# Expert lists in DRAM instead of one-hot products: a Mamba layer and a mixture of experts on one core

## The chip, the core and the metric

The kernel runs on one core of a Trainium2 chip. TensorE (PE; its weight loads are shown as PEld), VectorE (DVE), ScalarE (ACT), GpSimd (POOL) and SyncE (SP) run their own queues of instructions in order and wait for each other through semaphores. The metric is the device time of one execution in microseconds, the median of several runs. The profile comes from one more execution, whose own time is given beside it.

## The reference, cut to what matters

The input is one sequence of 4096 tokens of 256 numbers, all float32. A Mamba-like layer, a residual sum and a layer norm come first; then each token goes to one of 8 experts, chosen by the largest router logit, and a second residual sum and layer norm follow.

```python
xz = x @ W_in                                   # 4096 x 1024: conv_in, gated
conv = silu(conv1d(conv_in, conv_w) + conv_b)   # 4 taps, 512 channels
x_dbl = conv @ W_x                              # delta (1), B (16), C (16)
h = exp(delta * A) * h + delta * B * conv[:16]  # scan over the tokens, 16 states
y = (sum(h * C) + conv * D) * silu(gated)
x1 = layernorm(x + y @ W_out)

expert = argmax(x1 @ Wr.T + br)                 # one of 8 for each token
f = relu(x1 @ W1[expert].T + b1[expert]) @ W2[expert].T + b2[expert]
out = layernorm(x1 + f)
```

The kernel sorts the tokens by expert into blocks of up to 128 (some a little longer), so that each token passes through one expert alone.

## The kernel before, in words

**Rounds.** The tokens are cut into 8 blocks of 512 (`TB`). A block passes through a pipeline of steps, and the string `ROUND` gives the order in which one round emits them; `name.c:k` means step `name`, part `c`, for block `r - k` in round `r`. PE executes exactly in this order (its schedule is manual); the other engines' instructions are ordered by a scheduler by priority, and steps marked `@urgent` come ahead of others there. The steps:

- `project` (L748): product with W_in, 8 chunks of 128 columns, two PE products each (L763). ACT evicts chunks 0 to 3 into `xc` and `acc` (L780, L782), chunks 4 to 7 into `sg` (L778); later it makes `cv` from `acc` (L789).
- `taps` (L731): three DVE operations per chunk for the convolution (L734).
- `gauge` (L798): product with W_x (px, L805) and ACT's copy `pxs`. `gauge_out` (L813): four transposes (pxo, L819), an ACT copy and a chain of small DVE operations that ends in `sr` (L853, L856).
- `scan` (L861): transposes of `sr` (pt, L866), exponential on ACT, the scan on DVE (L870 to L881, ending in `parts_`).
- `gate` (L891): one product (py, L896), then for each of 4 chunks a DVE operation (L898) and a product with `sg` (L902), which is done by DVE for chunks 0, 2, 3 and by POOL for chunk 1 (for the last two blocks DVE does 0 and 3, POOL 1 and 2).
- `look`, `look_out` (L906, L923): the router's product with the rows and its transpose. `look_weights` does the same once with W_out.
- `project_out` (L939): four parts of four products (po, L943), residual sum (L947), squares (L951); after the last part the layer norm (L958 to L964) and the write of the rows to `x1d` in DRAM by SP (L968).
- `choose` (L972): nine small DVE operations that find the expert of each token. `rank` (L998): five small products and small DVE operations give each token a place `at` = expert x 4096 + its rank within the expert. Then one-hots are made: `colh` (L1027, DVE) and four `rowh` (L1032, POOL). `place` (L1038): eight products of 128x128 (pz, L1043) put the token numbers into `lists` in SBUF, which DVE adds up (L1047).
- `blocks_of` (L1052), after blocks 2, 4, 5 and 7, calls `table` (L307): from the counts (pn, L320) it works out on DVE which expert and which row of the lists each of 5, 8, 4 and 22 (with 5 lengthened ones) blocks has: `widx` for the weights (L453), and `pick` (L432), a one-hot of the list's row. `tokens_of` (L1062), one round later, calls `lookup` (L463): two products of `lists` with `pick` (pi, L468), an ACT copy (L473), two DVE operations, and `tidx`, the token numbers of the blocks.

**Expert blocks.** `blocks()` (L691) is a generator of the work of 32 blocks in quarters: `hidden` (ph, L598) twice and `close` (pe, L623) twice, with the transposes of the gathered rows (`turn`, pg, L566), the sum `xs` (L641) and `finish` (r, layer norm, y). From round 7 on the strings `QUARTERS` say how many quarters follow each step of a round; what remains comes after the last round. `prefetch` (L520) issues on POOL the indirect gather of a block's rows (xg, L515) and the indirect load of its expert's weights (we, L533; 128 rows of 4360 float32) into one of 3 buffers, up to two blocks ahead; `scatter` (L659) writes results to the output (L661). `turn(0)` stands in round 6 after `look_out`.

**Queues.** The indirect transfers all go through POOL's DMA queue. The 8 PSUM banks are three for `mm` (project, hidden), three for `o` (gate, project_out, close) and two for `tr` (all the rest).

Of the kernel before, what the change touches and what calls it, by code (L numbers as in the profile page):

```python
# [37 lines left out]
F32 = mybir.dt.float32  # L38
I32 = mybir.dt.int32
BF16 = mybir.dt.bfloat16  # L40
F16 = mybir.dt.float16
AF = mybir.ActivationFunctionType
ALU = mybir.AluOpType
AX = mybir.AxisListType
# [41 lines left out]

NM = NE + 1

O2 = DC * FF
OB = O2 + FC * D  # L90
OC = OB + FC
# [4 lines left out]


ROUND = """
    gauge:1 project.0:0 choose:3 gate:2 project.1:0 taps.0:0 tokens_of:4 look_weights:0
    project.2:0 taps.1:0 project.3:0 gauge_out:1 project_out.0:2 rank:3 taps.2:0  # L100
    project_out.1:2 project_out.2:2 taps.3:0 blocks_of:3 look:0 project.4:0 project.5:0
    look_out:1 project.6:0 scan:1 project_out.3:2 place:3 project.7:0
"""
ROUNDS = 13

QUARTERS = {
    7: "2211020000000200010200001000",
    8: "0001000000101100100000001101",
    9: "1000020000010000100000000110",
    10: "0000001000111000001100003002",  # L110
    11: "0000000000100000000000000000",
    12: "0000000000000000000010000000",
}

LOG_SERIES = (0.33333338, 0.19999444, 0.14308298, 0.1071537, 0.1214478)
# [3 lines left out]
def mamba_moe(  # L119
# [27 lines left out]
    def bank(tag, name, bufs=None):  # L147
        return ps.tile([P, 512], F32, tag=tag, name=name, bufs=bufs)


    x1d = dram.tile([T + 1, D], F32, name="x1d")


    st = {}
# [51 lines left out]
    def load_later():  # L206

        nc.sync.dma_start(wx[:, :, 0:XW], W_x.rearrange("(c p) n -> p c n", p=P))
        nc.sync.dma_start(al, A_log)
        nc.sync.dma_start(dp, D_param)  # L210
        nc.sync.dma_start(woutT, W_outT.rearrange("(c p) n -> p c n", p=P))
        nc.sync.dma_start(wout[:, :, 0:D], W_out.rearrange("(c p) d -> p c d", p=P))
        nc.sync.dma_start(brb, br.to_broadcast([P, NE]))
        nc.sync.dma_start(x1d[T : T + 1, :], lists[0:1, 0:D])

    eps = const.tile([P, 1], F32, name="eps")
    nc.gpsimd.memset(eps, EPS)
# [17 lines left out]
    back = iota([P, NE], [[-1, NE]], NE, 0, "back")  # L235
    part = iota([P, 1], [[0, 1]], 0, 1, "part")

    LH = NE * T // P // P
    lrow = iota([P, LH * P], [[P, LH * P]], 0, 0, "lrow", BF16)
    lcol = iota([P, P], [[1, P]], 0, 0, "lcol", BF16)  # L240
    prow = iota([P, LH], [[P * P, LH]], 0, P, "prow")
# [3 lines left out]
    code = const.tile([P, NT], F32, name="code")  # L245
    for base, at in ((1, 0), (-T // 2, NT // 2)):
        nc.gpsimd.iota(
            code[:, at : at + NT // 2], pattern=[[P, NT // 2]], base=base, channel_multiplier=1,
            allow_small_or_imprecise_dtypes=True,
        )  # L250
    lists = const.tile([P, LH * P], F32, name="lists")
    nc.gpsimd.memset(lists, 0.0)

    oneb = const.tile([P, P], BF16, name="oneb")
    nc.vector.tensor_copy(oneb, ones)
# [3 lines left out]
        channel_multiplier=-1,  # L259
# [47 lines left out]
    def table(b0, nb, columns, rows, early):  # L307


        def small(tag, shape, dtype=F32):  # L310
            return r1.tile([P, *shape], dtype, tag=tag, name=f"{tag}{b0}")
# [115 lines left out]
                row[:, nb:], row_of, float(P), blockoff[:, 0:longer], ALU.add, ALU.add  # L427
            )
        nc.vector.tensor_tensor(row[:, 0:nb], row[:, 0:nb], blockoff[:, 0:nb], ALU.add)
        pick = small("pick", [LH, nb + longer])  # L430
        for h in range(LH):
            nc.vector.tensor_scalar(pick[:, h, :], row, prow[:, h : h + 1], None, ALU.is_equal)  # L432
        eb = small("eb", [nb])
        nc.vector.tensor_reduce(eb, past, AX.X, ALU.add)
        if longer:
# [27 lines left out]
        def lookup():  # L463

            pi = bank("tr", f"pi{b0}", 2)
            n = nb + longer
            for h in range(LH):
                nc.tensor.matmul(  # L468
                    pi[:, 0:n], lhsT=lists[:, h * P : (h + 1) * P], rhs=pick[:, h, :],
                    start=(h == 0), stop=(h == LH - 1),  # L470
                )
            codes = small("codes", [n])
            nc.scalar.copy(codes, pi[:, 0:n])  # L473
            half = small("half", [n])
            nc.vector.tensor_scalar(half, codes, 0.0, -float(T + 1), ALU.is_gt, ALU.mult)
            tidx = const.tile([P, n], I32, name=f"tidx{b0}")
            nc.vector.scalar_tensor_tensor(tidx, codes, float(T), half, ALU.add, ALU.add)
            for b in range(nb):
                index[b0 + b] = rows, tidx[:, order(b0, b)]
            for b, x in LONG.items() if longer else ():  # L480
                further[b] = tidx[:, nb + x : nb + x + 1]
# [408 lines left out]
    @urgent  # L890
    def gate(i):  # L891
        cv, sg = st[i]["cv"], st[i]["sg"]


        py = bank("o", f"py{i}")
        nc.tensor.matmul(py, lhsT=oneb, rhs=upper(slice(0, P)), start=True, stop=True)  # L896
        for c in range(CC):
            nc.vector.scalar_tensor_tensor(  # L898
                cv[:, c, :], cv[:, c, :], dp[:, c : c + 1], py, ALU.mult, ALU.add
            )  # L900
            eng = nc.vector if c in ((0, 3) if i >= NB - 2 else (0, 2, 3)) else nc.gpsimd
            eng.tensor_tensor(sg[:, c, :], cv[:, c, :], sg[:, c, :], ALU.mult)  # L902

    rxs = {}
# [67 lines left out]
    def choose(i):  # L972
# [22 lines left out]
        nc.vector.tensor_tensor(earlier[:, i + 1, :], earlier[:, i, :], here, ALU.add)  # L995
        st[i]["oh"], st[i]["best"] = oh, best

    def rank(i):  # L998
        oh, best = st[i]["oh"], st[i]["best"]


        pr = bank("tr", f"pr{i}", 2)
        prv = pr[:, 0 : JT * NE]
        nc.tensor.matmul(
            prv, lhsT=trib, rhs=oh.rearrange("p j e -> p (j e)"), start=True, stop=False
        )
# [12 lines left out]
        at = a2.tile([P, JT], I32, tag="at", name=f"at{i}")  # L1019
        nc.vector.tensor_copy(at, best)  # L1020
        col = a2.tile([P, JT], I32, tag="col", name=f"col{i}")
        nc.vector.tensor_scalar(col, at, P - 1, None, ALU.bitwise_and)
        row = a2.tile([P, JT], F32, tag="row", name=f"row{i}")
        nc.vector.tensor_tensor(row, best, col, ALU.subtract)  # L1024
        rowh = a2.tile([P, JT, LH * P], F16, tag="rowh", name=f"rowh{i}", bufs=1)
        colh = a2.tile([P, JT, P], F16, tag="colh", name=f"colh{i}", bufs=1)
        nc.vector.tensor_tensor(  # L1027
            colh, lcol.unsqueeze(1).to_broadcast([P, JT, P]),
            col.unsqueeze(2).to_broadcast([P, JT, P]), ALU.is_equal,
        )  # L1030
        for j in range(JT):
            (nc.vector if i >= NB - 0 else nc.gpsimd).tensor_scalar(  # L1032
                rowh[:, j, :], lrow, row[:, j : j + 1],
                code[:, i * JT + j : i * JT + j + 1], ALU.is_equal, ALU.mult,
            )
        st[i]["rowh"], st[i]["colh"] = rowh, colh

    def place(i):  # L1038
        rowh, colh = st[i]["rowh"], st[i]["colh"]
        pz = bank("tr", f"pz{i}", 2)  # L1040
        for h in range(LH):
            for j in range(JT):
                nc.tensor.matmul(  # L1043
                    pz[:, h * P : (h + 1) * P], lhsT=rowh[:, j, h * P : (h + 1) * P],
                    rhs=colh[:, j, :], start=(j == 0), stop=(j == JT - 1),
                )
        nc.vector.tensor_tensor(lists, lists, pz[:, 0 : LH * P], ALU.add)  # L1047

    lookups = {}

# [16 lines left out]
    def have(i):  # L1067
# [5 lines left out]
    steps = dict(  # L1073
        project=project, taps=taps, gauge=gauge, gauge_out=gauge_out, scan=scan, gate=gate,
        look=look, look_out=look_out, project_out=project_out, choose=choose, rank=rank,
        place=place, blocks_of=blocks_of, tokens_of=tokens_of,
    )
    for r in range(ROUNDS):
        if have(r + 1):
# [75 lines left out]
```

## Time and profile before

| | |
|---|---|
| median of 3 runs | 474.22 us (473.63 to 474.29) |
| the profiled execution | 473.77 us, span 472.1 us |
| PE clock granted | 0.998 |
| busy share of the span | PE 97%, PEld 73%, DVE 69%, ACT 50%, POOL 40% |
| round from 99.8 to 126.2 us | PE 25.97 of 26.40 us, DVE 23.25, ACT 22.49, POOL 7.64 |
| expert blocks, 280 to 330 us | PE 49.63 of 50.00 us, DVE 30.94, POOL 25.56, DMA share 0.92, 342 GB/s |

A line of PE's waits has the waiting instruction, what ended the wait, then us in total, times, longest. A line of the timeline has start and length in us, engine, line, operation, tiles (out<-in), shape and count; PE's operations overlap, so what one costs is read from start to start. A line of the groups has count, busy us, mean ns of one, idle time before it and what ended that.

### The profile page before, as it was taken

How to read it: one execution, taken by the hardware profiler on the slowest of the kernel's cores; microseconds unless marked ns; L12 is line 12 of the kernel's file. 1: busy time of each engine (PE TensorE's matmuls, PEld its weight loads, DVE VectorE, ACT ScalarE, POOL GpSimd, SP SyncE). 2: the span in 40 equal slices, each digit the busy share in tenths (PEclk: the TensorE clock that was granted, in tenths of full speed). 3: DMA queues.
4: the chain of work that ended last, by engine and by line, in shares of the span. 5: the costliest groups of instructions: out<-in, count | busy, mean ns of one | idle time of the engine just before them, and what ended most of it. 6: DMA issues, size and time to landing. Idle time of an engine off the chain costs nothing.

```text
span 472.1 us, 7486 instructions
## 1 busy us (share of the span) xinstructions
PE 458.8 (97%) x2575; PEld 344.9 (73%) x2576; DVE 326.0 (69%) x1034; ACT 234.2 (50%) x513; POOL 190.1 (40%) x195
## 2 busy tenths in 40 slices
PE   8998999999999899999999999999999999999994
PEld 6343646464564567786888898999989898989884
DVE  2586969797999967984989679544556565645453
ACT  4687898879789784665754331221212121212111
POOL 3000101414154723450575655435436366645541
PEclk9999999999999999999999999999999999999999
DMA  8401012120408906714288499899996189967910
GB/s 247 162 0 46 0 46 89 43 92 1 135 1 345 376 25 206 282 34 184 47 288 279 191 309 356 303 354 345 339 361 248 47 281 357 293 246 248 361 37 22
DMA packets 23401, 89.98 MB, mean 191 GB/s; under 512 B 4914, under 2 KB 14909, under 8 KB 19650
## 3 DMA queue, kind: packets, MB, share of 16 engines
q0 software_dynamic: 8752, 74.71, 43.5%
q1 hardware_dynamic: 13650, 14.50, 9.3%
q8 instruction: 21, 0.34, 0.3%
q10 hardware_dynamic: 960, 0.27, 0.3%
q14 instruction: 18, 0.15, 0.1%
HBM read 87.78 MB, written 9.43 MB: 206 GB/s over the span
## 4 chain that ended last, share of the span: by engine, by line
PE 70%; DVE 17%; ACT 5%; issue 3%; DMA 3%; POOL 1%; POOLq 0%; ACTq 0%; DVEq 0%
PE ph L598 23%; PE pe L623 21%; PE pm L763 12%; PE po L943 7%; DVE acc L734 6%; DMA xg<-x1d,tidx 3%; PE px L805 2%; PE pf L634 1%; PE pg L566 1%; ACT acc L782 1%; DVE xb L947 1%; DVE hT L609 1%; DVE sg L902 1%; ACT xc L780 1%; PE pt L866 1%
## 5 line engine op out<-in xcount | busy, mean ns | idle before, releaser
L763 PE MATMUL pm<-xTb,win 128*128 128x512 f32 (+1 forms) x264 | 119.0, 589 | 0.0
L598 PEld LDWEIGHTS ph<-xgT,we 128*128 128x128 f32 x864 | 100.5, 192 | 3.9 <-DVE r L648 1.3
L598 PE MATMUL ph<-xgT,we 128*128 128x128 f32 x864 | 102.9, 276 | 0.1
L623 PE MATMUL pe<-we,hT 128*128 128x256 f32 x432 | 99.3, 380 | 0.7 <-DVE hT L609 0.7
L623 PEld LDWEIGHTS pe<-we,hT 128*128 128x128 f32 x432 | 79.3, 190 | 11.9 <-DVE hT L609 2.0
L763 PEld LDWEIGHTS pm<-xTb,win 128*128 128x128 f32 x264 | 48.0, 192 | 50.8 <-issue 48.0
L734 DVE SCALAR_TENSOR_TENSOR acc<-xc,cw,acc 128x512 f32<-128x512 f32 x96 | 70.1, 747 | 16.6 <-ACT acc L782 16.2
L285 ACT ACTIVATE sdm<-mvm,eps 128x1 f32<-128x1 f32 x32 | 9.4, 293 | 123.2 <-DVE mvm L283 123.2
L943 PE MATMUL po<-wout,sg 128*128 128x265 f32 x256 | 61.8, 389 | 0.3 <-POOL sg L902 0.3
L533 POOL DMA_INDIRECT we<-in_experts,widx x32 | 34.3, 1072 | 64.9 <-DVE r L648 37.5
L1032 POOL TENSOR_SCALAR rowh<-lrow,row,code 128x256 f16<-128x256 bf16 x32 | 43.9, 1378 | 25.0 <-DVE row L1024 17.9
L943 PEld LDWEIGHTS po<-wout,sg 128*128 128x128 f32 x256 | 46.8, 190 | 8.2 <-POOL sg L902 0.7
L661 POOL DMA_INDIRECT out<-y,tidx x32 | 33.4, 1043 | 44.5 <-DVE y L287 24.9
L609 DVE TENSOR_SCALAR hT<-ph,we 128x128 f32<-128x128 f32 x108 | 31.6, 342 | 25.3 <-PE ph L598 25.1
L902 POOL TENSOR_TENSOR sg<-cv,sg 128x512 f32<-128x512 f32 x10 | 15.7, 1573 | 76.9 <-DVE cv L898 76.8
L648 DVE TENSOR_TENSOR r<-pe,xs 128x256 f32<-128x256 f32 x32 | 13.5, 422 | 44.0 <-PE pe L623 44.0
L515 POOL DMA_INDIRECT xg<-x1d,tidx x32 | 33.2, 1038 | 24.3 <-PE pg L566 12.1
L607 ACT ACTIVATE hT<-ph,we 128x128 f32<-128x128 f32 x108 | 31.0, 366 | 19.6 <-PE ph L598 12.8
L780 ACT COPY xc<-pm 128x512 f32<-128x512 f32 x32 | 18.7, 583 | 21.3 <-PE pm L763 21.3
L782 ACT ACTIVATE acc<-pm,cb,cw 128x512 f32<-128x512 f32 x32 | 25.0, 781 | 0.0
L951 ACT ACTIVATE sta<-xb 128x256 f32<-128x256 f32 x32 | 16.1, 502 | 17.1 <-DVE xb L947 16.9
L947 DVE TENSOR_TENSOR xb<-po,xb 128x265 f32<-128x265 f32 x32 | 13.5, 425 | 15.3 <-PE po L943 15.2
(225 smaller groups left out, 616.0 us busy)
## 6 DMA issues: line engine op xcount, KB each, us to landing
xb<-in_x SPq DMA_DIRECT2D x8, 512.0 KB, 4.9
x1d<-x SPq DMA_DIRECT2D x8, 512.0 KB, 4.8
xTb<-in_xT SPq DMA_DIRECT2D x7, 512.0 KB, 3.7
win<-in_W_in SPq DMA_DIRECT2D x1, 512.0 KB, 5.1
we<-in_W_outT SPq DMA_DIRECT2D x1, 512.0 KB, 5.8
wout<-in_W_out SPq DMA_DIRECT2D x1, 512.0 KB, 6.8
we<-in_experts,widx POOLq DMA_INDIRECT x32
xg<-x1d,tidx POOLq DMA_INDIRECT x32
```

Of the source, the lines that this page charges most:

```text
L515: nc.gpsimd.indirect_dma_start(out=to, out_offset=None, in_=x1d[0:rows, :], in_offset=bass.IndirectOffsetOnAxis(ap=at, axis=0),)
L533: nc.gpsimd.indirect_dma_start(out=wes[n][:, :], out_offset=None, in_=experts, in_offset=bass.IndirectOffsetOnAxis(ap=weights[n], axis=0), ...
L598: nc.tensor.matmul(ph[:, n * w : (n + 1) * w], lhsT=we[:, at : at + P], rhs=xgT[:, dc * w : (dc + 1) * w], start=(dc == 0), stop=(dc == DC ...
L607: nc.scalar.activation(hT[:, fc, :], ph[:, n * w : (n + 1) * w], AF.Relu, bias=bias)
L609: last[b] = nc.vector.tensor_scalar(hT[:, fc, :], ph[:, n * w : (n + 1) * w], bias, 0.0, ALU.add, ALU.max)
L623: nc.tensor.matmul(py[:, 0:D], lhsT=hT[:, fc, 0:P], rhs=out_weights(fc), start=(fc == 0), stop=(fc == FC - 1),)
L661: moved = nc.gpsimd.indirect_dma_start(out=out, out_offset=bass.IndirectOffsetOnAxis(ap=at, axis=0), in_=rows, in_offset=None, bounds_chec ...
L734: nc.vector.scalar_tensor_tensor(acc, xc[:, c, k : k + TB], cw[:, c, k : k + 1], acc, ALU.mult, ALU.add)
L763: nc.tensor.matmul(banks[c][:, at], lhsT=win[:, dc, c * P : (c + 1) * P], rhs=xTb[:, dc, at], start=(dc == 0), stop=(dc == DC - 1),)
L782: evicted = nc.scalar.activation(acc, pm, AF.Identity, scale=cw[:, c, KC - 1 : KC], bias=cb[:, c : c + 1])
L943: nc.tensor.matmul(po[:, 0 : D + NM], lhsT=sg[:, c, j * P : (j + 1) * P], rhs=wout[:, c, :], start=(c == 0), stop=(c == CC - 1),)
L1032: (nc.vector if i >= NB - 0 else nc.gpsimd).tensor_scalar(rowh[:, j, :], lrow, row[:, j : j + 1], code[:, i * JT + j : i * JT + j + 1], AL ...
```

## The change

The lists move to DRAM. `lists` is a DRAM tensor of 257 rows of 128 words, filled once with the number 4096 (a row of zeros in `x1d`) by an SP transfer in `load_later`. `rank` ends with four indirect transfers from POOL, each of which writes 128 token numbers to the places `at`; they are declared free of order among themselves. The one-hots, `place` and its products are gone. `table` makes the number of the list's row on the partition of its block (three DVE operations) and issues on POOL an indirect gather of the rows, `entries`, one partition for each block. `lookup` turns them into float (`numbers`, DVE), transposes them on PE (pi) and copies them to `tidx` (DVE).

The steps of a round stand in a new order, `choose` belongs to the end of the round before, `rank` is urgent, `QUARTERS` is new, and there is one round less. The gate's product on POOL is chunk 0 instead of chunk 1, and for the last two blocks DVE does all four.

```diff
+    lists = dram.tile([LROWS * P, 1], I32, name="lists")
...
 ROUND = """
-    gauge:1 project.0:0 choose:3 gate:2 project.1:0 taps.0:0 tokens_of:4 look_weights:0
-    project.2:0 taps.1:0 project.3:0 gauge_out:1 project_out.0:2 rank:3 taps.2:0
-    project_out.1:2 project_out.2:2 taps.3:0 blocks_of:3 look:0 project.4:0 project.5:0
-    look_out:1 project.6:0 scan:1 project_out.3:2 place:3 project.7:0
+    project.0:0 gauge:1 gate:2 project.1:0 tokens_of:4 taps.0:0 gauge_out:1 taps.1:0
+    project.2:0 project.3:0 taps.2:0 project_out.0:2 taps.3:0 rank:3 project_out.1:2
+    project_out.2:2 blocks_of:3 look_weights:0 project.4:0 project.5:0 look_out:1
+    project.6:0 scan:1 project_out.3:2 choose:2 look:0 project.7:0
 """
-ROUNDS = 13
+ROUNDS = 12
...
-    7: "2211020000000200010200001000",
-    8: "0001000000101100100000001101",
-    9: "1000020000010000100000000110",
-    10: "0000001000111000001100003002",
-    11: "0000000000100000000000000000",
-    12: "0000000000000000000010000000",
+    7: "030001202020010100010001000",
+    8: "001000000010110110000000021",
+    9: "100001011000101000000001001",
+    10: "000000000000110000110000222",
+    11: "000100000000000000000000000",
...
+        nc.sync.dma_start(lists.rearrange("(p n) one -> p (n one)", p=P), noone)
...
-        pick = small("pick", [LH, nb + longer])
-        for h in range(LH):
-            nc.vector.tensor_scalar(pick[:, h, :], row, prow[:, h : h + 1], None, ALU.is_equal)
+        n = nb + longer
+        own = small("own", [n])[0:n, :]
+        nc.vector.tensor_tensor(own, row[0:n, :], ident[0:n, 0:n], ALU.mult)
+        line = small("line", [1])[0:n, :]
+        nc.vector.tensor_reduce(line, own, AX.X, ALU.add)
+        lineno = small("lineno", [1], I32)[0:n, :]
+        nc.vector.tensor_scalar(lineno, line, 1.0 / P, float(LROWS - 1), ALU.mult, ALU.min)
+        entries = small("entries", [P], I32)[0:n, :]
+        nc.gpsimd.indirect_dma_start(
+            out=entries, out_offset=None,
+            in_=lists.rearrange("(r c) one -> r (c one)", c=P),
+            in_offset=bass.IndirectOffsetOnAxis(ap=lineno, axis=0),
+        )
...
-            n = nb + longer
-            for h in range(LH):
-                nc.tensor.matmul(
-                    pi[:, 0:n], lhsT=lists[:, h * P : (h + 1) * P], rhs=pick[:, h, :],
-                    start=(h == 0), stop=(h == LH - 1),
-                )
-            codes = small("codes", [n])
-            nc.scalar.copy(codes, pi[:, 0:n])
-            half = small("half", [n])
-            nc.vector.tensor_scalar(half, codes, 0.0, -float(T + 1), ALU.is_gt, ALU.mult)
+            numbers = small("numbers", [P])[0:n, :]
+            nc.vector.tensor_copy(numbers, entries)
+            nc.tensor.transpose(pi[:, 0:n], numbers, ident[0:n, 0:n])
             tidx = const.tile([P, n], I32, name=f"tidx{b0}")
-            nc.vector.scalar_tensor_tensor(tidx, codes, float(T), half, ALU.add, ALU.add)
+            nc.vector.tensor_copy(tidx, pi[:, 0:n])
...
-            eng = nc.vector if c in ((0, 3) if i >= NB - 2 else (0, 2, 3)) else nc.gpsimd
+            eng = nc.vector if c in ((0, 1, 2, 3) if i >= NB - 2 else (1, 2, 3)) else nc.gpsimd
...
+    @urgent
     def rank(i):
...
-        nc.vector.tensor_tensor(
-            colh, lcol.unsqueeze(1).to_broadcast([P, JT, P]),
-            col.unsqueeze(2).to_broadcast([P, JT, P]), ALU.is_equal,
-        )
         for j in range(JT):
-            (nc.vector if i >= NB - 0 else nc.gpsimd).tensor_scalar(
-                rowh[:, j, :], lrow, row[:, j : j + 1],
-                code[:, i * JT + j : i * JT + j + 1], ALU.is_equal, ALU.mult,
-            )
-        st[i]["rowh"], st[i]["colh"] = rowh, colh
-
-    def place(i):
...
-                nc.tensor.matmul(
-                    pz[:, h * P : (h + 1) * P], lhsT=rowh[:, j, h * P : (h + 1) * P],
-                    rhs=colh[:, j, :], start=(j == 0), stop=(j == JT - 1),
-                )
-        nc.vector.tensor_tensor(lists, lists, pz[:, 0 : LH * P], ALU.add)
+            moved = nc.gpsimd.indirect_dma_start(
+                out=lists, out_offset=bass.IndirectOffsetOnAxis(ap=at[:, j : j + 1], axis=0),
+                in_=tokenno[:, i * JT + j : i * JT + j + 1], in_offset=None,
+            )
+
+            tc.declare_no_dep(moved.ins, group="lists", reason="tokens have no place in common")
+            tc.add_to_no_dep_group("lists", moved.ins)
```

More of the change, by code (lines that the diff above doesn't have):

```diff
@@ L40 @@
 BF16 = mybir.dt.bfloat16
-F16 = mybir.dt.float16
 AF = mybir.ActivationFunctionType
@@ L87 @@
 NM = NE + 1
+LROWS = NE * T // P + 1
 O2 = DC * FF
@@ L213, in load_later @@
         nc.sync.dma_start(brb, br.to_broadcast([P, NE]))
-        nc.sync.dma_start(x1d[T : T + 1, :], lists[0:1, 0:D])
+        nc.sync.dma_start(x1d[T : T + 1, :], parts_[P - 1 : P, 0:D])
+        nc.sync.dma_start(lists.rearrange("(p n) one -> p (n one)", p=P), noone)
     eps = const.tile([P, 1], F32, name="eps")
@@ L236, in mamba_moe @@
     part = iota([P, 1], [[0, 1]], 0, 1, "part")
[L238 to L241, printed above, removed]
     blockno = iota([P, NSB], [[P, NSB]], 0, 0, "blockno")
     blockoff = iota([P, NSB], [[P, NSB]], OFF, 0, "blockoff")
[L245 to L249, printed above, removed]
-        )
-    lists = const.tile([P, LH * P], F32, name="lists")
-    nc.gpsimd.memset(lists, 0.0)
+    tokenno = iota([P, NT], [[P, NT]], 0, 1, "tokenno", I32)
+    noone = iota([P, LROWS], [[0, LROWS]], T, 0, "noone", I32)
     oneb = const.tile([P, P], BF16, name="oneb")
@@ L1020, in rank @@
         nc.vector.tensor_copy(at, best)
[L1021 to L1026, printed above, removed]
-        nc.vector.tensor_tensor(
-            colh, lcol.unsqueeze(1).to_broadcast([P, JT, P]),
-            col.unsqueeze(2).to_broadcast([P, JT, P]), ALU.is_equal,
-        )
         for j in range(JT):
-            (nc.vector if i >= NB - 0 else nc.gpsimd).tensor_scalar(
-                rowh[:, j, :], lrow, row[:, j : j + 1],
-                code[:, i * JT + j : i * JT + j + 1], ALU.is_equal, ALU.mult,
-            )
-        st[i]["rowh"], st[i]["colh"] = rowh, colh
-    def place(i):
[L1039 to L1043, printed above, removed]
-                    pz[:, h * P : (h + 1) * P], lhsT=rowh[:, j, h * P : (h + 1) * P],
-                    rhs=colh[:, j, :], start=(j == 0), stop=(j == JT - 1),
-                )
-        nc.vector.tensor_tensor(lists, lists, pz[:, 0 : LH * P], ALU.add)
+            moved = nc.gpsimd.indirect_dma_start(
+                out=lists, out_offset=bass.IndirectOffsetOnAxis(ap=at[:, j : j + 1], axis=0),
+                in_=tokenno[:, i * JT + j : i * JT + j + 1], in_offset=None,
+            )
+            tc.declare_no_dep(moved.ins, group="lists", reason="tokens have no place in common")
+            tc.add_to_no_dep_group("lists", moved.ins)
     lookups = {}
@@ L1075, in mamba_moe @@
         look=look, look_out=look_out, project_out=project_out, choose=choose, rank=rank,
-        place=place, blocks_of=blocks_of, tokens_of=tokens_of,
+        blocks_of=blocks_of, tokens_of=tokens_of,
     )
```

## The prediction

> **What bounds the kernel now.** I read the page's busy shares first, then the waits of PE, then PE's timeline round by round.
>
> ```profile
> PE 458.8 (97%) x2575; PEld 344.9 (73%) x2576; DVE 326.0 (69%) x1034; ACT 234.2 (50%) x513; POOL 190.1 (40%) x195
> PE   8998999999999899999999999999999999999994
> ```
>
> PE is busy in every slice. Busy is not peak, so I looked for standing time in PE's waits:
>
> ```profile
> PE idle L225 <- POOL ident masks.py:199: 1.6, 1, 1.6
> PE pg L566 <- DMA xg<-x1d,tidx: 1.4, 1, 1.4
> PE py L896 <- DVE parts__145 L881: 1.2, 2, 0.9
> PE pt L866 <- DVE sr L856: 1.2, 3, 0.5
> PE pe L623 <- DVE hT L609: 0.7, 2, 0.4
> PE ph L598 <- DVE r L648: 0.6, 1, 0.6
> PE po L943 <- POOL sg L902: 0.3, 1, 0.3
> ```
>
> After its start PE stands 5.4 us in all; the last 6 us or so are the tail (last layer norm and scatter), which the change leaves alone. So the time is PE's sum of work: a product that leaves PE is a gain, and a new wait in front of a PE instruction is a loss.
>
> The stretch 99.8 to 126.2 is one round: PE 25.97 of 26.40 us, DVE 23.25, ACT 22.49. PE sets it; DVE and ACT have 3 to 4 us spare.
>
> **Removed from PE.** What a step costs is the distance from its first start to the next step's:
>
> ```profile
> 115.75 0.61 PE L1043 MATMUL pz<-colh,rowh 128*128 128x128 f16 x8
> 116.19 1.94 PE L763 MATMUL pm<-xTb,win 128*128 128x512 f32 x4
> ...
> 149.47 0.51 PE L468 MATMUL pi<-pick,lists 128*128 128x5 f32 x4
> 149.83 3.68 PE L763 MATMUL pm<-xTb,win 128*128 128x512 f32 x8
> ```
>
> `place`: 0.44 us, eight times: 3.5 us. Lookup products: 0.36 us, four times; in their place one transpose each, at most 0.11 (the two of pg take 0.38 in all and 0.21 to 0.22 start to start). Gain 4 x 0.25 = 1.0. Together 4.5 us that nothing hides.
>
> **Off DVE, ACT, POOL.** `rank` and `place` lose per round colh 0.68, lists 0.42, col and row 0.16 each on DVE: 1.4 us. Nothing on PE gets shorter by it, but it pays for what follows. POOL trades four rowh for four scatters a round:
>
> ```profile
> L661 POOL DMA_INDIRECT out<-y,tidx x32 | 33.4, 1043 | 44.5 <-DVE y L287 24.9 <-DVE hT L609 4.6 <-DVE spare L441 3.4
> L1032 POOL TENSOR_SCALAR rowh<-lrow,row,code 128x256 f16<-128x256 bf16 x32 | 43.9, 1378 | 25.0 <-DVE row L1024 17.9 <-DVE q L847 7.0
> ```
>
> No scatter of single words is in the trace; the nearest row is this scatter of 128 rows, 1.04 us plus the 0.3 us that POOL shows between two issues: 4 x 1.34 = 5.4 against 4 x 1.38 = 5.5. Bounds: 0.90 (the shortest scatter) to 1.82 us (the longest indirect issue, we), so -0.5 to +3 us of POOL per round. In rounds 3 to 5 nobody waits for it: POOL is busy 7.64 of 26.40 us there.
>
> The Trainium skill speaks against this ("SBUF — State Buffer", Who interferes with whom, and A bandwidth-pool intuition that's wrong): DVE and GpSimd share a port pair, and GpSimd writes no DMA descriptors while DVE holds it; it tells of a 620 ns DMA that took 3100 ns. By that figure four scatters would take about 12 us, the lookups would come some 7 us late each, and the kernel would be slower. The rows show a mild form: xg issues took 1.22 to 1.44 us beside a full DVE (153 to 159 us) against 0.97 at the median. I keep the rows.
>
> **New order of the steps.** `gauge_out` moves forward past project.2 and project.3 (3.4 us), with its ACT copies, its exp table load and 18 small DVE operations; `scan` stays after project.6. So pt, which waits for sr at the end of that chain, gets 3.4 us where it was at most 0.5 late: its 1.2 us go. Late next is py, which waits for DVE's scan chain; between pt and py now stands `look` too (0.57 us), so about half of its 1.2 us go: 0.6. `gauge` has project.0 ahead of it, whose evictions keep ACT busy before pxs; PE reaches the transposes of pxs 1.97 us (py and project.1) after px, the copy takes 0.58: hidden, and 0.6 us a round if ACT is two evictions behind. `choose` goes to the end of the round before, the same place on DVE (nine operations of 0.19 us, right behind the scan chain); `rank` turns urgent; `look` goes behind project_out. The gate's POOL product is chunk 0 instead of 1, and none for the last two blocks: two more DVE products of 0.77 us in each of rounds 8 and 9. The fill of the lists is one more transfer (132 KB) on SP ahead of load_rows; rows are wanted some 40 us later. Fewer rounds: the same quarters of expert work, in other places. All these: nothing on PE unless named.
>
> **The new wait.** Each lookup now goes scatters, gather of `entries`, copy `numbers` on DVE, transpose on PE, tidx, gather of xg. On POOL a weight load stands right before `entries`, and transfers of that queue land in order, as the trace shows for xg behind three weight loads. First stretches of time (their length, POOL busy, clock, DMA share, GB/s), then a line of the chain of waits:
>
> ```profile
> 142.00:143.00 1.00, 0.69 (x2) 1.00 0.00 0
> 143.00:146.00 3.00, 0.91 (x1) 1.00 0.91 291
> 146.00:149.00 3.00, 0.00 (x0) 1.00 1.03 439
> ...
> 153.01 12.19 DMA xg<-x1d,tidx
> ```
>
> A load (128x4360 f32, 2.23 MB) issued at 141.0 moves data from 143 to about 149: 8 us. So `entries` lands some 8.5 us after the load before it is issued, if the queue is empty then; 12.2 us is the other end. `numbers` stands in DVE's queue: while it waits, everything behind it (relus, gate) waits, and PE behind those. The four places, from pn on PE (start of the table), by the order in which the built program issues on each engine, with the durations above and 1.78 per half `hidden`, 1.73 per half `close`:
> - First (round 5 to 6): PE has 15.4 us between pn and the transpose. Scatters and load are issued by about 5.5, landing 14. Late 0 to 0.5; I take 0.3. In return xg0 is no longer behind three loads: turn(0) comes 13 us after the lookup, only one load is ahead of the gather; the 1.4 us go.
> - Second (7 to 8): PE 17.6 us, the load goes out when widx is ready, 3.3; landing 12, DVE is there at 11: 0.3.
> - Third (8 to 9): PE only 11.7 us. POOL has scatters, y3 and xg8 first, load at 3.5, landing 12: late 0.5. Then the gate of block 7, all on DVE: 4 x 0.74 + 4 x 0.77 = 6 us, PE has 5.4 us of other work: 0.9 with what DVE does before it.
> - Fourth (10 to 11): PE 16.2 us. Table on DVE 10 to 11 us (12.8 in the trace less colh and later relus), load at 6.7, landing 15.2: 0.2.
>
> Sum of new waits 2.2 us; bounds 0 and, at 12.2 us from issue to landing against some 6 us of cover each, 24.
>
> **The sum.** The profiled execution took 473.77 us (span 472.1 and 1.7 around it); the median of the three runs is 474.22, 0.45 above. Off: 4.5 products, 1.4 pg, 1.2 pt, 0.6 py = 7.7. On: 2.2, and 0.3 for evictions on ACT. 473.77 - 7.7 + 2.5 = 468.6; against the median 469.0. I forecast 468.6.
>
> **Rivals.**
> 1. Slower: `entries` comes late in all four places. Its place is numbers on DVE; it decides from 7.7/4 = 1.9 us beyond the cover, a landing 8 us after its own issue. For it: 12.19 us in the trace. Against: that one had two full loads and a part of a third ahead, these one. At 9.2 us, 3 late each: 473.8 - 7.7 + 12 + 1.2 (gate and evictions as above) = 479.3; at 12.2 us, 24 late in all, 491.3. Chance 0.18.
> 2. DVE or ACT sets rounds 3 to 6, so that PE's 0.44 and the pt stall are not given back there (4 x 0.9 = 3.6): 472.2. For it: DVE 88% busy in a fixed order. Against: DVE loses 1.4 a round, PE 0.44. Chance 0.14.
> 3. No wait is new: the covers suffice, and PE's 0.7 and 0.6 at pe and ph go with the table's relus: 464.8 to 466. Chance 0.13.
> 4. Gain and new waits cancel, or the transposes and copies merely take the products' place: 473.9. Chance 0.05.
> The forecast's own case, 466.5 to 471, has 0.50.
>
> **Numbers.** 0.2% is 0.95 us, about what can be told from no change. Faster: 0.50 + 0.14 + 0.13 = 0.77. Same 0.05, slower 0.18. The range reaches from case 3 to the milder part of rival 1: 464.5 to 476.
>
> **What would show it.** Right: rounds of about 25.5 us between 70 and 150; no wait of pg for xg; pt for sr gone; PE's new waits at pe, po or pi for DVE within 3 us; scatters near 1.0 us on POOL. Wrong: PE waits for numbers or hT of several us at the four lookups, DVE standing before the copy for `entries`; scatters of 2 us and more; rounds still at 26.4.

## The result: slower by 8.2%, and where it shows in the profile after

The changed kernel takes 512.8 us (median of 4 runs, 511.8 to 514.3) against 473.96 us of the kernel before (4 runs, 473.6 to 474.3): a ratio of 1.082, 95% interval 1.079 to 1.085. The forecast was 468.6. The profiled execution has a span of 512.5 us (before: 472.1) and a granted clock of 0.951 (before: 0.998).

First the page's busy shares, and PE and its granted clock in 40 slices:

```profile
PE 466.0 (91%) x2499; PEld 349.4 (68%) x2500; DVE 312.8 (61%) x1010; ACT 235.4 (46%) x510; POOL 174.7 (34%) x191
PE   8999999999938999994995996599999999999993
PEclk9999999999976999996997999679999999999998
```

PE has holes now, at 141, 231, 269 and from 307 to 333 us (a slice is 12.8 us), and in or behind each of them the clock is down. PE executes 76 operations fewer than before and is busy 7.2 us longer. PE's waits:

```profile
PE pi L471 <- DVE numbers L470: 14.1, 2, 10.5
PE px L801 <- DVE sda L955: 8.3, 1, 8.3
PE ph L594 <- DMA we<-in_experts,widx: 6.5, 1, 6.5
PE pi L471 <- DVE oh L988: 5.2, 1, 5.2
PE idle L228 <- POOL ident masks.py:199: 1.6, 1, 1.6
PE pe L619 <- DVE hT L605: 1.3, 2, 1.2
PE ph L594 <- DVE r L644: 0.7, 1, 0.7
PE py L892 <- DVE parts__139 L877: 0.4, 1, 0.4
PE pxo L815 <- DVE tidx L473: 0.3, 1, 0.3
```

After the start PE stands 36.8 us; before it was 5.4. The first four lines lie at the four lookups; the third is a wait for a weight load itself. The old waits, pg for xg and pt for `sr`, are gone. The 31.4 us more of waits and the 7.2 us more of busy time make 38.6 of the 40.4 us by which the span grew.

Next the first lookup in detail: POOL's timeline, then the rows of DVE and PE that follow (in brackets the idle time ahead of the instruction and what ended it).

```profile
133.37 0.96 POOL L1019 DMA_INDIRECT lists<-tokenno,at  x1 [0.31 <-issue]
134.64 1.05 POOL L529 DMA_INDIRECT we<-in_experts,widx  x1 [0.30 <-DVE left L463]
149.87 0.91 POOL L431 DMA_INDIRECT entries<-lists,lineno  x1 [14.18 <-issue]
155.95 0.22 DVE L470 CAST numbers<-entries 5x128 f32<-5x128 int32 x1 [11.65 <-DMA entries<-lists,lineno]
156.22 0.26 PE L471 MATMUL pi<-ident,numbers 5*128 5x5 f32 x1 [10.47 <-DVE numbers L470]
```

The last of the four scatters is issued at 133.37. POOL then stands 14.2 us in front of `entries` and issues it at 149.87; the rows are there at 155.95, 21.3 us after the weight load's issue at 134.64. Until then DVE stands 11.7 us and PE 10.5. POOL stands in the same way at all four lookups, 8.7 to 14.2 us each, 47.4 in all. Its wait is one for several things. What the profile names had long happened; what came last is the fourth scatter, whose last semaphore update is at 149.0 us and whose words the gather reads. Here is the group of the scatters, and their time from issue to landing (shortest, median, longest, of the 5 of 32 for which the trace pairs the two):

```profile
L1019 POOL DMA_INDIRECT lists<-tokenno,at x32 | 35.0, 1095 | 25.2 <-issue 7.0
DMA to landing us min/median/max: 8.2/14.4/18.9
```

On POOL a scatter takes what was forecast, about 1.0 to 1.1 us. It lands 14.4 us after its issue, at the median of those five.

The clock is the second part of the loss. These are stretches around the first stall (length, PE busy, granted clock, DMA share, GB/s):

```profile
137.00:142.00 5.00, 5.00 (x21) 1.00 1.00 38
145.00:150.00 5.00, 0.75 (x2) 0.81 0.53 84
150.00:156.00 6.00, 0.00 (x0) 0.50 1.00 398
157.00:163.00 6.00, 6.00 (x12) 0.61 0.98 390
163.00:168.00 5.00, 5.00 (x28) 1.00 0.69 212
```

While PE stands the clock goes to 0.50, and PE works on at 0.61 for the next 6 us: eight products of `project` take 5.79 us there (at 157.32) against 3.68 in a round (at 129.79). Stretches like these, at all four lookups, cost the 7.2 us more of busy time and the 4.5 us that the products off PE had saved by the prediction's figure, an estimate of 11.7 in all. The run without scatters below, with the same products, has PE busy 455.5 us, 10.5 less than here.

The gains are there too. A round between 99.0 and 124.2 us takes 25.20 us instead of 26.40, and PE is busy in all of it (length, busy time of PE, PEld, DVE, ACT and POOL, clock, DMA share, GB/s):

```profile
99.00:124.20 25.20, 25.20 (x98) 13.80 (x97) 21.60 (x60) 22.48 (x43) 6.94 (x6) 1.00 0.43 63
```

### The profile page after: what moved, and what is told of

Read it like the earlier page. It is cut to its first block, busy times and chain, and to the rows that moved or that the text cites. A ratio compares the mean times of both kernels' runs of the same rounds, so it can differ in the third digit from the quotient of the medians.

```text
span 512.5 us, 7308 instructions
## 1 busy us (share of the span) xinstructions
PE 466.0 (91%) x2499; PEld 349.4 (68%) x2500; DVE 312.8 (61%) x1010; ACT 235.4 (46%) x510; POOL 174.7 (34%) x191
## 5 line engine op out<-in xcount | busy, mean ns | idle before, releaser
L594 PEld LDWEIGHTS ph<-xgT,we 128*128 128x128 f32 x864 | 105.1, 200 | 11.8 <-issue 7.6
L594 PE MATMUL ph<-xgT,we 128*128 128x128 f32 x864 | 107.1, 284 | 6.5 <-DMA we<-in_experts,widx 6.5
L619 PE MATMUL pe<-we,hT 128*128 128x256 f32 x432 | 102.3, 389 | 1.3 <-DVE hT L605 1.3
L619 PEld LDWEIGHTS pe<-we,hT 128*128 128x128 f32 x432 | 82.3, 196 | 13.1 <-DVE hT L605 2.1
L730 DVE SCALAR_TENSOR_TENSOR acc<-xc,cw,acc 128x512 f32<-128x512 f32 x96 | 70.1, 744 | 14.8 <-ACT acc L778 14.4
L529 POOL DMA_INDIRECT we<-in_experts,widx x32 | 32.6, 1020 | 65.4 <-DVE r L644 28.1
L1019 POOL DMA_INDIRECT lists<-tokenno,at x32 | 35.0, 1095 | 25.2 <-issue 7.0
L511 POOL DMA_INDIRECT xg<-x1d,tidx x32 | 32.6, 1020 | 25.3 <-DVE tidx L473 11.7
L898 POOL TENSOR_TENSOR sg<-cv,sg 128x512 f32<-128x512 f32 x6 | 7.6, 1274 | 72.0 <-DVE cv L894 72.0
L801 PE MATMUL px<-cv,wx 128*64 128x512 f32 x64 | 17.2, 663 | 8.3 <-DVE sda L955 8.3
## 6 DMA issues: line engine op xcount, KB each, us to landing
lists<-tokenno,at POOLq DMA_INDIRECT x32, 14.4
```

The lines of the kernel that those rows point to most:

```text
L511: nc.gpsimd.indirect_dma_start(out=to, out_offset=None, in_=x1d[0:rows, :], in_offset=bass.IndirectOffsetOnAxis(ap=at, axis=0),)
L529: nc.gpsimd.indirect_dma_start(out=wes[n][:, :], out_offset=None, in_=experts, in_offset=bass.IndirectOffsetOnAxis(ap=weights[n], axis=0), ...
L594: nc.tensor.matmul(ph[:, n * w : (n + 1) * w], lhsT=we[:, at : at + P], rhs=xgT[:, dc * w : (dc + 1) * w], start=(dc == 0), stop=(dc == DC ...
L619: nc.tensor.matmul(py[:, 0:D], lhsT=hT[:, fc, 0:P], rhs=out_weights(fc), start=(fc == 0), stop=(fc == FC - 1),)
L730: nc.vector.scalar_tensor_tensor(acc, xc[:, c, k : k + TB], cw[:, c, k : k + 1], acc, ALU.mult, ALU.add)
L1019: moved = nc.gpsimd.indirect_dma_start(out=lists, out_offset=bass.IndirectOffsetOnAxis(ap=at[:, j : j + 1], axis=0), in_=tokenno[:, i * JT ...
```

## The experiments

Theory A: the scatters are the whole loss, by their landing. Its two forms are A1, POOL's wait for them in front of `entries`, and A2, the queue behind them. Rivals: R, the weight load ahead of the gather; O, the new order of the steps. Ratios below, with 95% intervals, are against runs of the kernel before on the same chip, whose medians were 479.4, 481.3, 480.5 and 474.3 us on the four chips used; absolute times of different chips are not compared.

### Which part costs: wait, scatters, or place of the lookup

**Second table.** The gather reads a table that SP fills and no scatter writes. In all runs with this table the token numbers are made up, so that other rows are gathered and the output is another.

```diff
+    ready = dram.tile([LROWS * P, 1], I32, name="ready")     # filled by SP once
...
-            in_=lists.rearrange("(r c) one -> r (c one)", c=P),
+            in_=ready.rearrange("(r c) one -> r (c one)", c=P),
```

> The changed kernel, but entries is gathered from a second table in DRAM that SP fills once and that no scatter writes, so the gather's issue waits for no scatter; the four scatters a round stay and go into the first table, which nobody reads. The token numbers are then made-up ones and the output is another. Theory A1 (the price is POOL's wait of 11 to 15 us in front of the gather until the scatters have landed): POOL no longer stands there, entries is issued within 2 us of the weight load, time 468 to 480 us. Theory A2 (the price is that whatever stands behind the scatters in POOL's queue lands only after them): entries lands as late as in the changed kernel, some 20 us after the first scatter, DVE still stands 5 to 11 us at numbers, time 500 to 514 us though POOL's wait is gone. Rival R (the 2.2 MB weight load in front of the gather is what it waits for): as A2, but entries lands 8 us after the weight load's issue, not 20.

Measured: 520.1 us, 1.0895 (1.0816 to 1.0975), no better than the changed kernel and 6 us above the range put down for A2. Again the timelines of POOL and DVE at the first lookup:

```profile
135.46 1.04 POOL L537 DMA_INDIRECT we<-in_experts,widx  x1 [0.31 <-issue]
137.54 0.91 POOL L439 DMA_INDIRECT entries<-ready,lineno  x1 [1.03 <-DVE lineno L437]
...
155.68 0.21 DVE L478 CAST numbers<-entries 5x128 f32<-5x128 int32 x1 [10.72 <-DMA entries<-ready,lineno]
```

POOL stands 1.0 us here instead of 14.2 (10.8 instead of 47.4 at all four lookups), the gather goes out 12 us earlier, and its rows come at the same moment, 155.7. So it is A2: what is issued behind the scatters lands after them. A1 falls as the whole reason: without the wait the price is the same.

**No scatters.** The same without the four scatters.

```diff
-        for j in range(JT):
-            moved = nc.gpsimd.indirect_dma_start(out=lists, ...)
```

> As the run with the second table, and without the scatters: the token lists are left out altogether, only the gather, numbers, transpose and what follows remain. Theories A1 and A2: 464 to 470 us, entries lands 8 to 10 us after the weight load's issue and PE's waits at pi, px and ph together are under 3 us. Rival R (weight load in front of the gather): PE still stands 3 us or more at each of four lookups, 480 us or more. Rival O (order of the steps): unchanged, above 500 us.

Measured: 472.8 us, 0.9862 (0.9840 to 0.9885), 3 us above the range put down for A1 and A2.

```profile
135.32 1.27 POOL L537 DMA_INDIRECT we<-in_experts,widx  x1 [7.52 <-DVE sr L860]
137.45 0.89 POOL L439 DMA_INDIRECT entries<-ready,lineno  x1 [0.85 <-DVE lineno L437]
...
145.55 0.21 DVE L478 CAST numbers<-entries 5x128 f32<-5x128 int32 x1 [0.68 <-DMA entries<-ready,lineno]
```

With the same weight load ahead, the rows are there 8.1 us after the gather's issue and DVE stands 0.7 us. R and O fall. Between the last two runs lie 47 us, which the scatters alone make.

**Later gather and lookup.** `entries` is issued where the lookup stood, the lookup comes behind the last taps, and the last round does ten quarters of expert work first.

```diff
-    project.0:0 gauge:1 gate:2 project.1:0 tokens_of:4 taps.0:0 gauge_out:1 taps.1:0
-    project.2:0 project.3:0 taps.2:0 project_out.0:2 taps.3:0 rank:3 project_out.1:2
+    project.0:0 gauge:1 gate:2 project.1:0 fetch:4 taps.0:0 gauge_out:1 taps.1:0
+    project.2:0 project.3:0 taps.2:0 project_out.0:2 taps.3:0 tokens_of:4 rank:3 project_out.1:2
```

> The changed kernel with all its work, but the gather of entries stands where the lookup stood (after project.1 of the next round) and the lookup itself (numbers, transpose, tidx) behind the last taps of that round; in the last round ten quarters of expert work come ahead of it. Theory A (scatters need about 15 to 20 us to land, and the lookup stands too near): the 36 us of PE's waits fall to under 6 us and the slow clock after them goes, 464 to 474 us. Rival R or O (weight load, order): above 490 us.

Measured: 518.3 us, 1.0813 (1.0787 to 1.0839). Theory A missed its own number; R and O had it, but fall by the run without scatters. The edit moved less than it was to move. PE's transpose stands later. On DVE, where urgent steps come ahead, the copy `numbers` still follows and precedes the same operations as in the changed kernel at all four lookups (at the first it stands between L990 and L991 here, between L985 and L986 there), and DVE still stands 24.8 us in front of it. At the first lookup:

```profile
155.82 0.21 DVE L475 CAST numbers<-entries 5x128 f32<-5x128 int32 x1 [10.46 <-DMA entries<-lists,lineno]
```

So a later place on PE alone brings nothing. Whether a copy that stands later on DVE would hide the landing was not tested.

### What makes a scatter slow

**Scatters added to the kernel before**, into a table that nobody reads, with the words packed as in the change or each 512 bytes from the next.

```diff
         nc.vector.tensor_copy(at, best)
+        nc.vector.tensor_scalar(far, best, 128.0, None, ALU.mult)      # second run only
+        for j in range(JT):
+            nc.gpsimd.indirect_dma_start(out=unread, out_offset=... at (or far) ..., in_=word)
```

> The kernel before, unchanged in order and products, with the four scatters of 4-byte words a round added behind at, into a table in DRAM that nobody reads, at the places of the changed kernel. If the packed words alone are the cost, whatever the order of the steps and with no lookup through DRAM: weight loads, xg and out behind them land late, PE waits for them, 1.03 to 1.09 of the kernel before. If the loss needs the new order or the lookup's chain: 1.00 to 1.02.

> The same addition to the kernel before, with every word 512 bytes from the next. If neighbouring words are what costs, this one is near the kernel before: 1.00 to 1.025 (POOL's 32 issues of some 1.3 us and a small operation on DVE a round stay). If scatters of words cost by their number: as the run with packed words.

Measured: packed 515.1 us, 1.0889 (1.0828 to 1.0950); apart 499.8 us, 1.0539 (1.0492 to 1.0586). The DMA part of the page (count, median us from issue to landing), packed and then apart; the medians are of those issues whose landing the trace pairs, 5 and 13 of the 32 scatters, 3 and 10 of the 32 weight loads:

```profile
unread<-word,at POOLq DMA_INDIRECT x32, 16.7
we<-in_experts,widx POOLq DMA_INDIRECT x32, 15.1
```

```profile
unread<-word,far POOLq DMA_INDIRECT x32, 2.6
we<-in_experts,widx POOLq DMA_INDIRECT x32, 10.2
```

The same words land in 2.6 us when they lie apart and in 16.7 when they lie side by side. No new order and no lookup through DRAM is needed for that. But the time of the packed run is not all the words' doing, and the run with words apart missed its forecast, for one reason: in both the scatters stand ahead of the `rowh` on POOL, and the placing products wait for these. Packed, then apart:

```profile
PE pz L1052 <- POOL rowh L1041: 13.8, 15, 1.1
```

```profile
PE pz L1054 <- POOL rowh L1043: 15.1, 18, 1.1
```

So what the packing costs here is the difference of the two runs, some 15 us, and not the whole 41. It shows as PE's waits for gathered rows (pg for xg, 7.6 us against 1.9) and for a weight load (ph, 3.0 us against none), and as slow clock.

Nor is it POOL's queue alone that is held. SP's transfer of a block of the input, `xTb`, issued at 124.9 us, lands 9.6 us after its issue with packed words; issued at 125.5 us with words apart it lands after 3.7. In the changed kernel the one issued at 114.9 us takes 11.0 us, against 3.2 before (118.2 us).

**Words apart, wider rows.** The run with the second table again, with the scatters changed only: 4-byte words 512 bytes apart; rows of 64 bytes; rows of 512 bytes.

```diff
-    lists = dram.tile([LROWS * P, 1], I32, name="lists")
+    lists = dram.tile([LROWS * P, 16], I32, name="lists")              # or 128
...
-                in_=tokenno[:, i * JT + j : i * JT + j + 1], in_offset=None,
+                in_=noone[:, 0:16], in_offset=None,                    # or 128
```

> As the run with the second table, still 128 single words of 4 bytes in each scatter, but every word goes to a place of its own 512 bytes from the next (the index is multiplied by 128, the table 128 times as long). Theory S-neighbours (words that fall into one stretch of DRAM wait for each other): quick, 474 to 485 us. Theory S-size (a 4-byte write is slow wherever it goes) and rival C: four scatters still need 15 us or more, 510 to 525 us.

> As the run with the second table (the gather reads a table that no scatter writes, token numbers made up), but each scatter writes 128 rows of 64 bytes instead of 128 single words of 4 bytes, into a table of 64-byte rows that nobody reads. Theory S (single words are slow to write because they are so small, or lie together in one stretch of DRAM): four scatters land within 8 us instead of 15 to 20, time 474 to 485 us on the scale of that run's 520. Rival C (what costs is the count of rows, whatever their size): as that run, four scatters in 18 us or more, 510 to 525 us.

> As the run with 64-byte rows, with rows of 512 bytes. Theory S in the form that a write below 512 bytes is a read and a write: only here the scatters become quick, four within 6 us, time 473 to 480 us, and 64-byte rows stay slow. Theory S in the form that only single words or neighbours are slow: here and with 64 bytes the same. Rival C (count of rows): 510 to 525 us.

Measured: apart 488.4 us, 1.0124 (1.0061 to 1.0187); 64 bytes 487.4 us, 1.0133 (1.0059 to 1.0207); 512 bytes 485.5 us, 1.0098 (1.0057 to 1.0139), against 1.0895 with packed words. The times are 2 to 6 us above the ranges put down for quick scatters and over 20 below the rival's 510 to 525. In all three the first gather's rows come about 8 us after its issue, as without scatters. So neither the count of the writes nor their small size is slow by itself; single words side by side are. The Trainium skill ("DMA: Bandwidth & Descriptors", Specifications) says that transfers under 512 bytes are done by reading and writing back; between 64 and 512 bytes these runs show no difference.

**The change mended: rows of 32 bytes.** The whole computation and the wait for the scatters, with rows of 8 words of which the first is the token's number; the second run also has the later lookup.

```diff
-    lists = dram.tile([LROWS * P, 1], I32, name="lists")
+    lists = dram.tile([LROWS * P, 8], I32, name="lists")
...
-            nc.vector.tensor_copy(numbers, entries)
+            nc.vector.tensor_copy(numbers, entries[:, :, 0])
```

> The changed kernel with its whole work and its wait for the scatters, but the table has rows of 8 words (32 bytes), a scatter writes 32 bytes a token (the token number first), and entries gathers 4 KB a line, of which numbers takes every eighth word. If what was slow is single words lying next to each other, the scatters land within 3 us each, POOL's wait in front of the gather falls from 11 to 15 us to under 3, and the time is 1.005 to 1.02 of the kernel before, as in the runs with 64 and 512 bytes. If 32 bytes still share what makes neighbours slow: 1.04 to 1.08.

> The run with 32-byte rows, and the gather and the lookup stand later, as in the run that put them later. With quick scatters the later place leaves cover for what is late at the third and fourth lookup: 0.985 to 1.005 of the kernel before. If what remains is POOL's time or the queue's, not the lookups: as the run with 32-byte rows alone, 1.005 to 1.02.

Measured: 485.8 us, 1.0126 (1.0052 to 1.0200), the time as forecast; later lookup 492.2 us, 1.0249 (1.0180 to 1.0317), a miss. In the mended run the scatters issued at 129.9, 131.5, 132.8 and 134.2 us have their last semaphore updates at 132.3, 133.6, 135.0 and 136.2, so each lands within 2.5 us. The run's waits of POOL in front of `entries`:

```profile
POOL entries L433 <- DVE hT L607: 3.4, 1, 3.4
POOL entries L433 <- DVE lineno L431: 1.2, 1, 1.2
POOL entries L433 <- issue: 0.6, 2, 0.3
```

47.4 us have become 5.2, and the ratio is that of the three runs that did not wait for the scatters at all, 1.010 to 1.013: with quick scatters the dependence through DRAM costs no more than these intervals, some 0.7% to either side, can hide. The Trainium skill asks for that wait ("DMA: Bandwidth & Descriptors", Rules for kernel authors: a DMA that reads what another wrote waits for the other's completion), which the trace of the change shows POOL doing. With quick scatters the later gather and transpose do harm; on DVE the copy again stands in the same place at the first three lookups.

**POOL's time alone.** No scatters, but four POOL products of 128x256 in their place.

> The run without scatters (second table, token lists left out), with four POOL products of 128x256 in the place of the four scatters of a round, some 1.2 to 1.4 us each. It asks what the 12 us are that quick scatters (64 or 512 bytes, or words apart) still cost against none. Theory P (POOL's time: weight loads, xg and out are issued later): 1.005 to 1.015 of the kernel before. Theory Q (the transfers in the queue): as without scatters, 0.983 to 0.992.

Measured: 476.6 us, 0.9924 (0.9890 to 0.9959): between the two forecasts. POOL's time takes 0.6% (0.2 to 1.0) of the 2.6% that lie between the mended run and none. The other 2%, which the three runs with quick scatters and a second table have as well, go with the transfers of the scatters, and these runs do not tell how.

### The order of the steps

**New order, products kept.** The kernel before with the new order, quarters, urgent `rank` and gate; `place` behind `scan`, then behind project.5, then behind `gauge` of the next round.

```diff
-    project.6:0 scan:1 project_out.3:2 choose:2 look:0 project.7:0
+    project.6:0 scan:1 project_out.3:2 place:3 choose:2 look:0 project.7:0
```

> The kernel before with everything of the change except the lists in DRAM: the new order of a round, choose one round earlier, the urgent rank, the new quarters of expert work, the gate's product of chunk 0 on POOL. One-hots, eight placing products and the lookup products stay (place stands after scan). Theory A (the scatters and the gather behind them are the whole loss, the order is a gain): rounds of 25.2 us as in the changed kernel plus 0.44 for the products, 25.6; time 467 to 472 us, no wait of PE above 1.5 us. Rival O (the new order and its quarters cost the time): 490 us or more, with PE waiting several us at the lookups. Rival N (the order brings nothing by itself): 473 to 475 us.

> The first run again (products kept, new order of the steps), with place moved forward behind project.5, so that the product of look no longer waits for a PSUM buffer that DVE's sum into lists holds (6.1 us in that run). If that position was the loss there, the new order itself is a gain: 0.985 to 0.997 of the kernel before. If the order itself costs: 1.01 and more, as in that run.

> The first run again (products kept, new order of the steps), with place in the round after, behind gauge, where POOL's rowh have had half a round and no product of look follows at once. If the new order is a gain by itself and the two runs before lost by place's position only: rounds of 25.6 us and 0.985 to 0.998 of the kernel before. If the order itself costs: 1.01 and more.

Measured: 486.7 us, 1.0170 (1.0131 to 1.0208); 500.9 us, 1.0391 (1.0341 to 1.0442); 492.7 us, 1.0237 (1.0151 to 1.0322). The first fits none of its forecasts; the other two have the value put down for an order that costs by itself. Against that stands the run without scatters, which has this order and is faster than before. The largest wait of PE that goes with `place`, one line from each run:

```profile
PE prx L913 <- DVE lists L1047: 6.1, 4, 2.1
```

```profile
PE pz L1043 <- POOL rowh L1032: 11.6, 12, 1.6
```

```profile
PE pi L467 <- DVE lists L1047: 6.3, 1, 6.3
```

Either the products come before their `rowh`, or their sum into `lists` holds up the next user of the PSUM buffer or the lookup. That this is the whole loss is argued from the waits, not shown. The order is fitted to a round without `place`; there, in the runs without or with quick scatters, rounds take 25.2 us.

**One step alone.** Only `gauge_out` moves forward, in the kernel before; the quarters stay behind the same steps.

```diff
-    project.2:0 taps.1:0 project.3:0 gauge_out:1 project_out.0:2 rank:3 taps.2:0
+    gauge_out:1 project.2:0 taps.1:0 project.3:0 project_out.0:2 rank:3 taps.2:0
```

> The kernel before with one step of the new order alone: gauge_out moves forward past project.2 and project.3, so that sr is ready before pt. The prediction put 1.2 us of PE's waits on that. If so: 0.996 to 0.999 of the kernel before and the wait of pt for sr gone. If ACT or DVE pays it back elsewhere: 0.999 to 1.003.

Measured: 473.8 us, 0.9983 (0.9967 to 0.9999). The wait of pt for `sr` (1.2 us) is gone, and the gain is some 0.8 us. It is the only version with the whole computation that is not slower than the kernel before, and its gain is less than a single run can tell.

## Why the prediction was wrong

**The step that failed** is the price of the scatters. The prediction took the nearest row, the scatter of results, and bounded the scatters by their time on POOL, 0.90 to 1.82 us. That was right (0.99 us at the median, 1.53 at most). But it priced the issue alone. Their landing was given no term; "so `entries` lands some 8.5 us after the load before it is issued, if the queue is empty then" carried the condition that failed. The queue was not empty: the four scatters of a round kept it busy for some 15 us after the last was issued. Nor was it only the order of one queue, on which the prediction built: SP's transfers were late too. The landing of a row scatter could not stand in for it either, because what makes the words slow is that they are neighbours, and no row of the trace before has that.

**The new waits** were 2.2 us in the forecast. Measured are 36.8 us of waits less the 5.4 of before, and some 11 us of slow clock on top, for which the forecast had no term. Its upper bound of 24 us, from 12.2 us between issue and landing, was too low: 21.3 us passed at the first lookup. Without scatters the same steps gave about what was forecast: DVE stood 2.9 us for `entries` at all four lookups together, and at the first the rows came 10.2 us after the issue of the weight load ahead (forecast 8.5).

**The gains held**, as a sum. Rounds were to take about 25.5 us and took 25.2; the waits of pg and pt vanished. With POOL's work in place and no scatters the kernel was 0.76% (0.41 to 1.10%) faster than before, 3.6 us; without that work 1.38%, 6.6 us. The forecast was 5.2. The single terms were not measured one by one. Of the 44 us between forecast and measurement some 33 go with the words' being neighbours (1.082 of the time before against 1.013 with rows of 32 bytes), some 10 with the quick scatters that are left (1.013 against 0.992), and under 2 with all the rest (0.992 against the forecast's 0.989). These ratios come from different chips.

**The rivals.** Rival 1 named the place (`numbers` on DVE, all four lookups) and the sign, at a chance of 0.18, and its worst price, 491.3, was 21.5 us too low; it gave the weight load as the reason, where the runs show the scatters. Of the "wrong" signs listed, the waits of PE and DVE at the four lookups appeared; scatters of 2 us and more on POOL, and rounds still at 26.4, did not. The Trainium skill's figure for the shared port ("SBUF — State Buffer", A bandwidth-pool intuition that's wrong) gave the right sign for another reason: scatters that stand in the issue, which the trace does not show (1.53 us at most). The prediction's lower bound for POOL, -0.5 us a round, is -0.7 by its own numbers; nothing rests on it.

**Left open**: why neighbouring words wait for each other; whether it is their nearness or the small table that they all fall into (132 KB packed, 1 MB with rows of 32 bytes, 17 MB with words apart), which no run tells apart; how long the stretch is that they share (4-byte words side by side are slow, 32-byte rows side by side are not); a lookup that stands later on DVE; and the 2% that quick scatters still cost.

## What to carry to other kernels

Price a new transfer twice, for the engine that issues it and for its landing, and look for what is issued behind it and beside it: here the issue was 1 us and the landing 14, weight loads stood behind, and SP's transfers were late too. Do not scatter single words to neighbouring places in DRAM without measuring it; here a row of 32 bytes for each was enough to make them quick. When a bound engine gets a new wait, add the slow clock that follows a stall to its price.

## What was not expected of the hardware

- 128 words of 4 bytes, scattered to places side by side, need about 5 us, and scatters in a row do so one after another: in the semaphores' updates of the trace three issued at 103.8, 105.5 and 106.7 us are complete at 109.9, 115.4 and 121.1. With words 512 bytes apart a scatter lands in 2.6 us.
- The slow words hold back other transfers. In the stretch from 137 to 142 us, shown above, 38 GB/s are moved at a DMA share of 1.00: the packets that start there are the weight load's, 17,440 bytes each, and take 5.8 to 9.0 us, against 0.65 us at the median of the run.
- At `entries` the profile names "issue" or an old event as the end of POOL's long waits. It was the landing of the scatters: the last update of the fourth is at 149.0 us, the gather goes out at 149.87, and at a table that no scatter writes the wait at the first lookup is 1.0 us.
